# Eight-layer graph network on one core: layer norm by node tile, tied weight loads, stores within a recurrence and by tile

## The chip, the cores and the metric

The kernel runs on one core of a Trainium2 chip, as one launch. Its time is the device time in microseconds. Before the change the median of three runs is 5691.67 us (5687.64 to 5693.42). One further execution was profiled; every duration below is from that one.

The core has five engines with an instruction stream each, worked off in order: PE (matrix products, with PEld loading its weights), DVE (vector), ACT (scalar functions), POOL and SP. SP, ACT and POOL also issue DMAs, which run on 16 DMA engines; SP and ACT have a hardware queue each, POOL a software queue. A tensor in on-chip memory has up to 128 partitions; matrix products are written to PSUM.

## The reference

x is 625 x 512 (float32), with a graph of 20000 edges sorted by destination. Eight layers follow one another, each as

```
x = x + layer(_layernorm(x))      # (x - mean) / sqrt(var + 1e-5), no scale, no shift
```

with these layers:

- l0_gnn: Chebyshev graph convolution, eight terms through a dense 625 x 625 Laplacian.
- l0_ffn: one of 16 experts, picked by the mean over all nodes.
- l1_gnn: graph convolution of width 128, gathered over the edges, then 128 to 512.
- l1_ffn: 8 experts, gates by eight Sinkhorn rounds, each expert for its top nodes.
- l2_gnn: 32 relations made of 8 bases; `h_rel = einsum('ni,rio->rno', x, weight)`, then gathered over the edges.
- l2_ffn: a recurrence over the 625 nodes as time steps:

```
logits = concat(h, c, x_t) @ W_sel.T + b_sel
s = argmax(logits)                                # one of S = 4 weight sets
g = x_t @ W_ih[s].T + h @ W_hh[s].T + b_ih[s] + b_hh[s]
i, f, g, o = split(g, 4)
c = sigmoid(f) * c + sigmoid(i) * tanh(g);  h = sigmoid(o) * tanh(c)
```

- l3_gnn: two layers of graph attention with four heads, then a linear layer.
- l3_ffn: attention over the nodes with 8 heads, in one of three variants picked by the mean over the nodes.

## The kernel before

**Tiles.** The 625 nodes are NT = 5 tiles of P = 125 partitions. x stays on chip as `self.x`, 125 x 5 x 512. The stages run in the order of the layers; a scheduler orders the instructions of each engine by their dependences and puts in the semaphores. A DMA takes one of 8 semaphores in turn and waits for the DMA that had it last. Three loops (edge counts, the two gathers of l1_gnn and l2_gnn, the recurrence) are ordered by hand in a `tile_critical` block. At the beginning of such a block every engine waits for all DMAs that stand ahead of it in the program, whatever they load.

**Layer norm.** `layer_norm` (L39 to L55) stands at the head of each layer: bn_stats and bn_aggr for each tile (DVE, L46, L47), one square root for all five tiles (ACT, L48), one reciprocal (L49), then a subtract and multiply for each tile (L51). Its tiles come from a pool of the layer. After it `transpose_nodes` (L57) turns the nodes by 20 PE transposes (L63), copied from PSUM by DVE (L64). l0_ffn and l3_ffn also take the mean over nodes by 40 small products (L373, L1276).

**Loads on ACT's queue.** l1_ffn issues the 8 bases of l2_gnn, 1 MB each, from ACT at its beginning (L471). l2_gnn issues 16 small DMAs of comb from ACT (L588).

**l2_gnn.** It multiplies xT by the 8 bases (L608), brings the result into another layout by node_basis DMAs (L619), multiplies it by comb (L634) and stores the relation table to DRAM by 40 stores on SP (L643, L647). The gather (L681 on) is a `tile_critical` block: POOL issues 160 indirect loads of 125 table rows (L688), DVE makes a one-hot matrix for each (L692), PE adds up (L216). Then x is added (L700).

**Loads of the recurrent weights.** Memory for four sets of W_hh, 4 MB each (whh0 to whh3), is set aside ahead of the gather (L660). `load_set` (L703) loads a set by four DMAs of 1 MB. Sets 0 to 2 go by SP, drawn from a generator among the stores of gin. whh3 first serves as the double buffer of W_ih (`load`, L747 to L752): each column block of W_ih is 2 MB, two DMAs from ACT. Set 3 itself is loaded at the end by POOL, half after each of the last two column blocks. None of these loads depends on the relation table, so the scheduler puts them as early as memory and semaphores allow.

**gin** (l2_ffn, L779 to L877) computes the input products of all four sets for all nodes. It has 8 column blocks times 5 tiles, 40 units. A unit is 16 products and two of the bias on PE (L847, L849) into one of three PSUM buffers, then ACT's sigmoid and tanh for the cell's guess (L812 to L815), and a split of the sum into three bf16 parts: ACT casts (L737), DVE subtracts (L738), ACT casts (L739), DVE subtracts (L740). The parts stand in gxo3 (pool of three buffers) and go to DRAM as gxp, 750 KB for each unit, by SP (L860). PE transposes the guess of unit u - 1 after the products of unit u (L824). At the end, the logits' part of the input (xl3) is stored to gxp from ACT, five DMAs of 19 KB (L878). Padding zeros of gxp are stored by POOL in `setup` (L92).

**Recurrence** (L891 to L1097): a `tile_critical` block of 625 steps. SP loads a row of gxp for each step (L1092) into gs, PE adds it and h times W_hh[s] (L955, L964), DVE and ACT compute the cell.

**End.** `store` (L281) writes x to `out` by one DMA on SP.

The lines of the steps that follow are these; the scheme of a unit of gin is the heart of it:

```
ps = psum.tile([P, 2, D], F32, name="gx_ps")
...
rest = p2.tile([P, 2, 2, 256], F32, name="rest", bufs=1)
o3 = p3.tile([P, 3, 2, 2, 256], BF16, name="gxo3")
summands(lambda q: o3[:, q].rearrange("p s q n -> p q s n"),
         ps.rearrange("p q (s n) -> p q s n", n=256), rest)
nc.sync.dma_start(gxp[t * P : (t + 1) * P, c // 2, :, at : at + 2 * D],
                  o3.rearrange("p r s q n -> p r (s q n)"))
```

Of the kernel before, what the change touches and what calls it, by code (L numbers as in the profile page):

```python
# [8 lines left out]
F32 = mybir.dt.float32  # L9
# [20 lines left out]
class _Kernel:  # L30
# [8 lines left out]
    def layer_norm(self, pool):  # L39
        nc, x = self.nc, self.x  # L40
        st = pool.tile([P, NT, 6], F32, name="ln_st")
        mv = pool.tile([P, NT, 2], F32, name="ln_mv")
        rs = pool.tile([P, NT], F32, name="ln_rs")
        xn = pool.tile([P, NT, D], F32, name="ln_x")
        for t in range(NT):
            nc.vector.bn_stats(st[:, t, :], x[:, t, :])  # L46
            nc.vector.bn_aggr(mv[:, t, :], st[:, t, :])  # L47
        nc.scalar.activation(rs, mv[:, :, 1], AF.Sqrt, bias=self.eps)  # L48
        nc.vector.reciprocal(rs, rs)  # L49
        for t in range(NT):  # L50
            nc.vector.tensor_scalar(  # L51
                xn[:, t, :], x[:, t, :], mv[:, t, 0:1], rs[:, t : t + 1],
                op0=ALU.subtract, op1=ALU.mult,
            )
        return xn  # L55
# [11 lines left out]
    def setup(self, ctx):  # L67
# [7 lines left out]
        self.eps = const.tile([P, 1], F32, name="eps")  # L75
        nc.vector.memset(self.eps, 1e-5)
# [10 lines left out]
        zero = const.tile([P, DC - 1, 3, 26], BF16, name="zero")  # L87
        nc.gpsimd.memset(zero, 0.0)
        self.graph()
        for t in range(NT):  # L90
            for j in range(1, DC):
                nc.gpsimd.dma_start(self.gxp[t * P : (t + 1) * P, j, :, 2048:], zero[:, j - 1])  # L92

    def graph(self):
# [53 lines left out]
        with tc.tile_pool(name="graph", bufs=1) as pool, tc.tile_pool(  # L148
# [38 lines left out]
            for t in range(NT):  # L187
                nc.scalar.copy(self.count[:, t, :512], main[t])
# [92 lines left out]
    def store(self):  # L281
        self.nc.sync.dma_start(self.out.rearrange("(t p) c -> p t c", p=P), self.x)


    def l0_gnn(self):
        tc, nc, a, x = self.tc, self.nc, self.a, self.x
        K = 8
        with ExitStack() as ctx:
# [3 lines left out]
            xn = self.layer_norm(pool)  # L292
# [33 lines left out]
            for k in range(K - 1, -1, -1):  # L326
# [10 lines left out]
                for t, ps in enumerate(sums):  # L337
# [6 lines left out]
                    if k == 0:  # L344
                        nc.vector.tensor_add(x[:, t, :], ps, x[:, t, :])
                    elif k == 1:
# [11 lines left out]
    def l0_ffn(self):  # L358
        tc, nc, a, x = self.tc, self.nc, self.a, self.x
        NE = 16  # L360
        with tc.tile_pool(name="sw", bufs=1) as pool, tc.tile_pool(
# [6 lines left out]
            xn = self.layer_norm(pool)  # L368
# [33 lines left out]
            for t in range(NT):  # L402
                ps = psum.tile([P, D], F32, name="y_ps")
                for c in range(DC):
# [4 lines left out]
                                               op0=ALU.mult, op1=ALU.add)  # L409


    def l1_gnn(self):
        tc, nc, a, x = self.tc, self.nc, self.a, self.x
        H = 128
        with tc.tile_pool(name="gc", bufs=1) as pool:
# [8 lines left out]
            xn = self.layer_norm(pool)  # L424
# [23 lines left out]
            with tc.tile_pool(name="gc_ps2", bufs=2, space=PSUM) as psum, tc.tile_pool(  # L448
                name="gc2", bufs=2
            ) as p2:  # L450
                for t in range(NT):
# [7 lines left out]
                    nc.vector.tensor_add(x[:, t, :], ps, x[:, t, :])  # L459

# [111 lines left out]
    def l2_gnn(self):  # L572
# [88 lines left out]
        with tc.tile_pool(name="rs", bufs=1) as pool:  # L661
# [7 lines left out]
            with tc.tile_pool(name="rel_in", bufs=1) as sp, tc.tile_pool(  # L669
# [29 lines left out]
                for t in range(NT):  # L699
                    nc.vector.tensor_add(x[:, t, :], acc[t], x[:, t, :])  # L700
# [759 lines left out]
```

## Time and profile before

| what | value |
|---|---|
| median of three runs | 5691.67 us (5687.64 to 5693.42) |
| the profiled execution | 5684.2 us |
| its span | 5682.4 us |
| mean granted TensorE clock | 0.952 of full speed |
| PE busy | 5001.1 us (88%) |
| DVE busy | 2527.0 us (44%) |
| ACT busy | 957.8 us (17%) |
| POOL busy | 422.5 us (7%) |
| first gate product of the recurrence | 1971.58 us |
| first addition of its result to x | 5102.87 us |

Times of the timeline count from the start of the span. A row of the timeline is: start, duration (us), engine and line, operation, output <- inputs, shapes, count, and in brackets the idle time before it with what ended that. A row of waits is: who waited (engine, tile, line) <- for whom, us in all, times, the longest. A row of a stretch is: its bounds, its length, busy time of PE with its instructions, the granted clock, the busy share of the DMA engines, and GB/s. A row of a group is: busy us, mean ns of one, then the idle time of the engine ahead of it with what ended it. PE counts as busy while it works at half clock too.

### The profile page before, as it was taken

Reading aid. Unit: us, or ns where it says so; the run is one execution under the profiler, and the core shown is the slowest. Engines: PE = TensorE matmul, PEld = TensorE weight load, DVE = VectorE, ACT = ScalarE, POOL = GpSimd, SP = SyncE. Lnnn points to the kernel's source line nnn. Section 1 sums busy time; section 2 is a strip of 40 time slices with the busy share of each in tenths; the row PEclk is TensorE's granted clock in tenths of the full one; section 3 lists DMA queues with packets and bytes.
Section 4 is the critical chain, followed back from the end, with each engine's and each line's share of the span. In section 5 each row is a group of like instructions: output and inputs, shape, how many; then the busy total and the mean of one; then the engine's idle time right before and its main releaser. Section 6 shows DMA issues by size and latency. Waiting matters only on the chain.

```text
span 5682.4 us, 173043 instructions
## 1 busy us (share of the span) xinstructions
PE 5001.1 (88%) x74317; PEld 3028.8 (53%) x74318; DVE 2527.0 (44%) x10296; ACT 957.8 (17%) x3300; POOL 422.5 (7%) x361
## 2 busy tenths in 40 slices
PE   6898879885799789898999999999999898988987
PEld 2444764321244356565666666666666565665544
DVE  6312436334333344444444454444545444456514
ACT  1000001120023211111111111111111111114314
POOL 1000760006700000000000000000000000000000
PEclk8798998988999899999999999999999999998989
DMA  1100121396554400000000000000000000001000
GB/s 15 46 30 14 41 67 66 93 286 172 152 143 156 116 10 11 10 11 10 11 10 10 10 11 11 11 10 11 11 11 11 11 10 10 9 23 49 15 32 10
DMA packets 153754, 247.87 MB, mean 44 GB/s; under 512 B 58875, under 2 KB 61572, under 8 KB 151462
## 3 DMA queue, kind: packets, MB, share of 16 engines
q1 hardware_dynamic: 83850, 163.27, 9.6%
q0 software_dynamic: 50288, 56.13, 4.0%
q10 hardware_dynamic: 19372, 25.52, 1.6%
q8 instruction: 115, 1.88, 0.1%
q14 instruction: 129, 1.06, 0.1%
HBM read 160.50 MB, written 73.72 MB: 41 GB/s over the span
## 4 chain that ended last, share of the span: by engine, by line
PE 53%; DVE 6%; issue 3%; DMA 2%; PEld 1%; ACT 1%; PEldq 0%; SPq 0%; ACTq 0%; DVEq 0%
PE gate_if L964 21%; PE gate_o L964 9%; PE gate_g L964 9%; DVE to L1076 3%; PE gate_if L955 3%; PE idle L972 2%; DMA gs<-gxp 2%; PE o_ps L1203 2%; PE o_ps L1137 2%; PE big_ps L1312 1%; PE gate_g L955 1%; PE gate_o L955 1%; PE big_ps L1332 1%; PE fc_ps L1243 1%; PE blk_ps L1193 1%
## 5 line engine op out<-in xcount | busy, mean ns | idle before, releaser
L964 PE MATMUL gate_if<-whh,h 128*32 128x256 f32 x21664 | 1348.6, 387 | 2.1 <-issue 2.1
L964 PEld LDWEIGHTS gate_if<-whh,h 128*32 128x32 f32 x21664 | 599.8, 109 | 368.3 <-DVE h L1080 129.2
L964 PE MATMUL gate_g<-whh,h 128*32 128x128 f32 x19968 | 672.2, 275 | 0.0
L964 PE MATMUL gate_o<-whh,h 128*32 128x128 f32 x19968 | 659.2, 273 | 0.0
L1067 DVE STREAM_TRANSPOSE tif<-gate_if 128x256 f32<-128x256 f32 x625 | 281.3, 450 | 837.7 <-PE gate_g L964 834.0
L964 PEld LDWEIGHTS gate_g<-whh,h 128*32 128x32 f32 x19968 | 520.8, 110 | 171.6 <-issue 162.6
L964 PEld LDWEIGHTS gate_o<-whh,h 128*32 128x32 f32 x19968 | 557.7, 110 | 0.0
L1059 ACT ACTIVATE sd<-tif 128x8 f32<-128x8 f32 x625 | 134.7, 216 | 2120.1 <-DVE tif L1067 2120.1
L955 PE MATMUL gate_if<-gs,pick 128*128 128x256 bf16 x678 | 192.7, 284 | 135.5 <-DVE to L1076 47.1
L847 PE MATMUL gx_ps<-whh,xT 128*125 128x512 f32 x640 | 299.9, 612 | 0.3 <-DVE xls L787 0.3
L216 PE MATMUL acc<-msg,dst_w 125*125 125x512 f32 x352 | 193.8, 659 | 105.0 <-DMA msg<-rel_table,row_i 95.3
L1068 DVE STREAM_TRANSPOSE tg<-gate_g 128x128 f32<-128x128 f32 x625 | 198.0, 317 | 160.2 <-PE gate_g L964 160.2
L258 PE MATMUL acc<-msg,dst_w 125*125 125x128 f32 x1600 | 210.7, 282 | 44.0 <-DMA msg<-conv_table,src_i 37.8
L250 POOL DMA_INDIRECT msg<-conv_table,src_i x160 | 196.1, 1226 | 609.3 <-issue 607.2
L688 POOL DMA_INDIRECT msg<-rel_table,row_i x160 | 195.9, 1224 | 537.5 <-issue 519.6
L1076 DVE STREAM_TRANSPOSE to<-gate_o 128x128 f32<-128x128 f32 x625 | 198.1, 317 | 67.1
L258 PEld LDWEIGHTS acc<-msg,dst_w 125*125 125x125 f32 x1600 | 188.3, 190 | 66.4 <-issue 55.2
L1024 PE MATMUL logits<-gs,three 128*2 128x5 bf16 x624 | 103.5, 166 | 129.0 <-issue 50.0
L1088 DVE MAX8 mx<-logits 2x8 f32<-2x8 f32 x624 | 100.8, 162 | 246.4 <-PE logits L1036 246.4
L972 PE MATMUL idle<-hot 128*128 128x384 bf16 x624 | 204.8, 328 | 0.0
L1024 PEld LDWEIGHTS logits<-gs,three 128*2 128x2 bf16 x624 | 49.3, 79 | 289.7 <-DMA gs<-gxp 229.8
L216 PEld LDWEIGHTS acc<-msg,dst_w 125*125 125x125 f32 x352 | 59.1, 198 | 240.6 <-issue 191.3
(356 smaller groups left out, 6150.9 us busy)
## 6 DMA issues: line engine op xcount, KB each, us to landing
rel_table<-h_rel SPq DMA_DIRECT2D x39, 1024.0 KB
gs<-gxp SPq DMA_DIRECT2D x625, 48.6 KB
gxp<-gxo SPq DMA_DIRECT2D x40, 750.0 KB
whh<-in_L_ffn_W_ih ACTq DMA_DIRECT2D x16, 1024.0 KB
whh<-in_L_ffn_W_hh SPq DMA_DIRECT2D x12, 1024.0 KB
node_basis<-by_basis SPq DMA_DIRECT2D x39, 256.0 KB
ch_wk<-in_L_gnn_weight SPq DMA_DIRECT2D x8, 1024.0 KB
expert<-in_L_ffn_experts SPq DMA_DIRECT2D x8, 1024.0 KB
```

What stands on the lines that cost most here:

```text
L216: m = PE.matmul(out, lhs, rhs, start=False, stop=False, skip_group_check=True)
L250: nc.gpsimd.indirect_dma_start(out=m, out_offset=None, in_=table, in_offset=bass.IndirectOffsetOnAxis(ap=index[:, c : c + 1], axis=0),)
L258: nc.tensor.matmul(acc[t][:, :width], w1[:, t * P : (t + 1) * P], m, start=c == 0, stop=c == EC - 1)
L688: get = nc.gpsimd.indirect_dma_start(out=msg[:, i, :], out_offset=None, in_=table, in_offset=bass.IndirectOffsetOnAxis(ap=idx[:, c : c + 1 ...
L847: nc.tensor.matmul(ps[:, q], xT[:, k, t * P : (t + 1) * P], w[:, q, k, :], start=k == 0, stop=False)
L955: m = PE.matmul(out[:, : hi - lo], pick, gs[:, s * D + lo : s * D + hi], start=True, stop=last, skip_group_check=True)
L964: yield PE.matmul(out[32 * j : 32 * j + 32, : hi - lo], h[:, b : b + 1].to_broadcast([128, 32]), self.whh[s][:, b, j, lo:hi], start=False, ...
L972: PE.matmul(idle[:, :cols], hot[:, :128], hot[:, :cols], start=True, stop=True)
L1024: after(PE.matmul(lg[:, :LG], three[:, 0], gs[:, S * D : S * D + LG], start=True, stop=False), s_gx, rows)
L1067: after(DVE.transpose(tif, IF[:, :256]), s_if, t + 1).then_inc(s_v)
L1068: after(DVE.transpose(tg, G[:, :128]), s_g, t + 1).then_inc(s_v)
L1076: after(DVE.transpose(to, O[:, :128]), s_o, t + 1).then_inc(s_v)
```

## The change

- `layer_norm` becomes `norm(t)`, for one tile, with one square root and one reciprocal each. It is called in the layer ahead, right after the addition that completes x of that tile; the five of the first layer are called within `graph`. Its tiles are allocated once, for the whole kernel.
- The padding zeros are stored in l1_ffn by the source. In the order of POOL's instructions they stand where they stood.
- Two small DMAs read the end of the relation table into whh3 (from ACT) and whh0 (from SP), ahead of the loads into these sets, so that those loads can only follow the table's last stores.
- In gin, `rest` uses the memory of xn, and gxo3 has two buffers.
- Set 3 of W_hh is loaded by ACT's queue instead of POOL's.
- The logits' part xl3 is stored from POOL within the recurrence's block; each store waits for the one before, and SP waits for a tile's store before it loads that tile's first row.
- The output is stored by tile, after each tile's last addition.
- In l1_ffn, three instead of two held expert results are added after each product of a later expert.

```diff
-    def layer_norm(self, pool):
...
+    def norm(self, t):
+
         nc, x = self.nc, self.x
+        st, mv, rs = (v[:, t] for v in self.moments)
+        nc.vector.bn_stats(st, x[:, t, :])
+        nc.vector.bn_aggr(mv, st)
+        nc.scalar.activation(rs, mv[:, 1:2], AF.Sqrt, bias=self.eps)
         nc.vector.reciprocal(rs, rs)
+        nc.vector.tensor_scalar(self.xn[:, t, :], x[:, t, :], mv[:, 0:1], rs, op0=ALU.subtract, op1=ALU.mult)
...
                     if k == 0:
                         nc.vector.tensor_add(x[:, t, :], ps, x[:, t, :])
+                        self.norm(t)
...
-                for _ in range(2):
+                if e == NE - 1:
+                    self.norm(t)
+                for _ in range(3):
...
+        nc.scalar.dma_start(self.whh[3][0:1, :, 0, :2], table[N * R - 1 :, : 2 * DC].rearrange("p (q n) -> p q n", q=DC))
+        nc.sync.dma_start(self.whh[0][:, 0, 0, :1], table[N * R - 128 :, :1])
...
-                p3 = gin.enter_context(tc.tile_pool(name="gin3", bufs=3))
+                p3 = gin.enter_context(tc.tile_pool(name="gin3", bufs=2))
...
-                        rest = p2.tile([P, 2, 2, 256], F32, name="rest", bufs=1)
+                        rest = self.xn[:, :2].rearrange("p q (s n) -> p q s n", n=256)
...
-                        list(self.load_set(S - 1, slice(2 * (c % 2), 2 * (c % 2) + 2), nc.gpsimd))
+                        list(self.load_set(S - 1, slice(2 * (c % 2), 2 * (c % 2) + 2), nc.scalar))
...
-                for t in range(NT):
-                    nc.scalar.dma_start(gxp[t * P : (t + 1) * P, 0, :, 4 * D :], xl3[:, :, t])
-            hist = self.recurrence(ctx, wl, gxp)
+            hist = self.recurrence(ctx, wl, gxp, xl3)
...
+            for t in range(NT):
+                d = nc.gpsimd.dma_start(gxp[t * P : (t + 1) * P, 0, :, 4 * D :], xl3[:, :, t])
+                if t:
+                    after(d, s_xl, 16 * t)
+                d.then_inc(s_xl, 16)
             for t in range(N):
+                if t % P == 0:
+                    SP.wait_ge(s_xl, 16 * (t // P + 1))
                 d = SP.dma_start(gs[: 3 * DC, :], gxp[t].rearrange("j q g -> (j q) g"))
...
                 nc.vector.tensor_add(x[:, t, :], ps[:, :D], x[:, t, :])
+                nc.sync.dma_start(self.out[t * P : (t + 1) * P, :], x[:, t, :])
```

The calls of `norm(t)` in the other layers follow the last addition to x in the same way (L408, L459, L700, L885, L1246 of the kernel before).

## Prediction

> **What bounds the kernel now.** I read the chain of work that ended last first, then the costliest groups, to learn which engine the time hangs on.
>
> ```profile
> PE 53%; DVE 6%; issue 3%; DMA 2%; PEld 1%; ACT 1%; PEldq 0%; SPq 0%; ACTq 0%; DVEq 0%
> ...
> L964 PE MATMUL gate_if<-whh,h 128*32 128x256 f32 x21664 | 1348.6, 387 | 2.1 <-issue 2.1
> ...
> L847 PE MATMUL gx_ps<-whh,xT 128*125 128x512 f32 x640 | 299.9, 612 | 0.3 <-DVE xls L787 0.3
> ```
>
> The end hangs on TensorE. L964 is the recurrence, 1971.6 to about 5100 us; none of its steps is edited, so 3130 us stay as they are. The gain or loss must come from the 2550 us around it. There I asked for the waits of PE between 1036 and 1260 us and, in a second answer, between 512 and 600 us:
>
> ```profile
> PE tr_ps L63 <- DVE ln_x L51: 11.3, 1, 11.3
> ```
>
> ```profile
> PE tr_ps L63 <- ACT dinv L275: 7.1, 1, 7.1
> ...
> PE mean_ps L373 <- DVE ln_x L51: 5.9, 1, 5.9
> ```
>
> Each is PE standing idle (us in all, times, longest) while a layer norm runs between the last addition to x and the next layer's transposes. The timeline of DVE shows how the longest comes about:
>
> ```profile
> 1035.35 0.75 DVE L560 SCALAR_TENSOR_TENSOR x<-y_ps,sel,x 125x512 f32<-125x512 f32 x1 [2.68 <-PE y_ps L491]
> 1036.02 0.68 DVE L46 BATCH_NORM_STATS2 ln_st<-x 125x6 f32<-125x512 f32 x1
> ...
> 1045.71 0.19 DVE L49 RECIPROCAL ln_rs<-ln_rs 125x5 f32<-125x5 f32 x1 [6.09 <-ACT ln_rs L48]
> 1045.93 2.37 DVE L51 TENSOR_SCALAR ln_x<-x,ln_mv,ln_rs 125x512 f32<-125x512 f32 x5
> ```
>
> x is complete at 1036.1, but the one square root stands on ACT behind 16 DMA issues of comb (1037.0, 8.3 us) and the statistics of all five tiles.
>
> **1. Layer norm by tile.** The order of instructions of the changed kernel puts four of the five tiles' norms beside the previous layer's matmuls. Behind the last x there remain statistics 0.66, aggregate 0.17, root 0.30, reciprocal 0.19, scaling 0.5 and two handovers between engines: an estimate of 2.3 us. Layer by layer, from the idle time of PE and the copies that DVE must still do:
> - l0_ffn: PE starts at 512.2 and is busy to 522. Now the last scaled tile is there at about 509, and four tiles' transposes fill the wait: **-5**.
> - l1_gnn: PE starts at 566.0 after 7.1 idle and works through 20 transposes and 40 matmuls to 576.4. It can start at 559.0, and its own 10.6 us of work then end near 569.6: **-6.5**.
> - l1_ffn: the root waits behind 8 issues of bases (838.9, 13.6 us); PE starts at 853.8 after 14.9 idle. In the new order the roots precede most issues; DVE's five additions and norms (1.9 us each from 834.3) and four copies end near 846, while PE has transposes from 840: **-11**. The cost moved is that bases 3 to 8 are issued later; they are first read at 1052.7, 200 us on.
> - l2_gnn: last tile ready at 1039.2 (copies between), matmuls on bases at 1041 in place of 1052.7: **-11.5**. Fifteen comb issues now come after the roots and end about 1047; the first reader comes only after 1080.
> - l2_ffn: DVE is the limit on both sides (five additions and norms are 9.4 us from 1567.0, to 1577; before, the last scaling ended at 1576.7): **-1**.
> - l3_gnn: DVE again: in the new order counts and negations stand between the norms, and adding up its rows from 5101.3 gives the last copy at 5121 against 5120.7: **0**.
> - l3_ffn: the 40 mean matmuls (8.5 us) end at 5461.7, now near 5456.5: **-5**.
> - l0_gnn: its norm hid in DVE's idle time at 186 to 194 us. Four statistics, three aggregates, two reciprocals and two scalings (3.9 us) now precede the graph stage, on a DVE chain from 18.1 to 28.6 that starts it; that chain has some 2.5 us of gaps: **+2**.
>
> Together **-38**. The bounds are -26 (half of the two large ones) and -44. The four extra roots and reciprocals of each layer lie beside matmuls. Here the clock matters too:
>
> ```profile
> 1046.00:1050.00 4.00, 2.95 (x13) 0.50 0.10 1
> 1050.00:1054.00 4.00, 3.23 (x11) 0.50 0.00 0
> 1054.00:1058.00 4.00, 4.00 (x7) 0.66 0.00 0
> 1058.00:1062.00 4.00, 4.00 (x10) 1.00 0.00 0
> ```
>
> The column ahead of the last two (DMA share, GB/s) is the granted clock: after the idle stretch PE works about 10 us at half speed, and the 17 matmuls from 1052.7 take 9.55 us, where 17 x 0.43 = 7.3 would do. I count nothing for this, since gaps of 2 to 3 us remain. The Trainium skill (TensorE: Matmul & The Clock Gate, "What's actually happening") has the clock halved after an idle window of about 3.4 us and restored after as long a busy one; the rows agree with a halving, and by its window most of the shortened gaps would keep the clock.
>
> **2. Ties of the loads.** W_ih's four loads (4 MB, ACT) were issued from 1268.2, ahead of the table's landing at about 1276.7. DVE and POOL enter the gather at 1302.5, held by those loads and two W_hh loads of SP; in the new order this barrier still holds for all of them. Their transfer starts some 5 to 7 us later, behind a small DMA that waits for the table. One W_hh load (5 us) has no tie and fills that time, the DMAs were at a share of 1.0 before too, and the second W_hh load no longer waits for the first W_ih: **+1.5**. Ends: -2 (a freer table) and +6 (the whole delay). The zero stores stand at the same place of POOL's order: 0.
>
> **3. Two gxo3 buffers in place of three.** Behind 40 units of 8.4 us of matmuls (L847, to 1939.5) ACT waits 39.5 us in 13 times for the landing of a store, so that three buffers were already short:
>
> ```profile
> 1730.24 0.38 ACT L813 ACTIVATE th<-gx_ps 125x256 bf16<-125x256 f32 x1
> 1741.40 1.01 ACT L737 CAST gxo<-gx_ps 125x1024 bf16<-125x1024 f32 x1 [10.78 <-DMA gxp<-gxo]
> ```
>
> Behind this waiting cast stand the cell's tanh and product, and PE's transpose waits for those 5.83 us, until 1743.93. A store of 750 KB takes 6.6 us (116 GB/s, DMA share 0.33, at 1928 to 1936); a buffer is held for 4.6 (write) + 2.3 (issue to first packet) + 6.6 = 13.5 us, under two units' 16.8. Alone, two buffers would do, with 3.3 us to spare. But from 1637 to 1800 the same queue carries five W_hh loads of about 5 us, and W_ih's 2 MB per column (8 us of all DMAs) slow it. PE's lead over the queue shrinks by one unit, 8.4 us, in each burst that uses it up; and when ACT waits, the queue runs dry for 4.6 + 2.3 - 6.6 = 0.3 us per unit, about 13 times. One burst: 8.4 + 4 = **+13** (rounded up, since the first loads come one store earlier in the new order). Ends: 0 (bursts stay inside the 3.3) and +25 (a second and third burst). The Trainium skill (DMA: Bandwidth & Descriptors, "Why a DMA increments its semaphore by 16 and not by 1") speaks against the change: a DMA from SP or ACT is spread over the largest number up to 16 that divides the slowest dimension, 5 for 125 rows. The share of 0.33 agrees with 5 of 16, so a store gains nothing from idle DMAs.
>
> **4. Start of the recurrence.**
>
> ```profile
> 1946.19 0.29 DVE L740 TENSOR_TENSOR xl<-less,xl 125x125 bf16<-125x125 f32 x1 [0.36 <-ACT xl L739]
> 1966.06 0.17 DVE L924 TENSOR_REDUCE quarter<-ident 128x4 f32<-128x12 f32 x1 [19.58 <-DMA gxp<-xl]
> ```
>
> Last gx matmul 1939.5, barrier 1966.1, first gs load 1969.5, first gate 1971.6. The barrier no longer holds for the logits' stores, but for the last gxo store and the W_hh set. Four W_hh issues on ACT (0.5 to 1 us each) now stand between the last unit's casts, so the last store is written near +9 after the last matmul and shares the DMAs with 2 MB: landed at +19 in place of +26.6. Then POOL's first store (about 2.4 from the barrier to its issue, as SP's row shows, and 6.2 to land, the median of the 15 zero stores of the same 19 KB on POOL) holds SP's first load: +28, against +30. **-1.5**; ends -8 and +5. The later four stores land within 40 us and are needed only every 125 steps of 5 us.
>
> **5. Output by tile.** The one store is issued at 5669.5 and ends the span at 5682.4: 12.9 us, at 128 GB/s. The additions are 3.4 us apart, a tile needs 250 KB / 128 GB/s = 2.0 us, so nothing queues up; the last one ends in 12.9 - 10.2 + 2.0 = 4.7, at most 6.9 after its issue: **-6** (ends -8, -4).
>
> **Sum**: -38 + 1.5 + 13 - 1.5 - 6 = -31. The profiled execution took 5684.2 (span 5682.4), giving 5653. The median of the runs is 5691.67, 7.5 above it, so I put the forecast at 5661.
>
> **The rivals.**
> - *Gin hides it, and the clock stays up.* Stores of 13.5 us fit into 16.8, and four of the gaps no longer lose some 2 us each to the cold clock (9.55 - 7.3 above): part 3 at 0 and -8 beside: 5640. For it: outside 1637 to 1800 ACT never waits. Against: 13 waits with three buffers. By the Trainium skill's window, cited above, the clock part would come out so.
> - *Given back downstream.* Half the gain of part 1 vanishes since l1_ffn has 11.6 us of idle PE later anyway (waiting for DVE at 984 to 996) and the table's stores run at a DMA share of 0.9: -31 + 19 = -12: 5680. Against: the chain in l1_ffn is DVE's, and it starts earlier too.
> - *Slower: two buffers throttle the whole saturated stretch.* If a store's 14 to 20 us from write to landing (units 5 to 22) come from crowded DMAs and not from its own queue, a pair of units takes 4.6 + 20 = 24.6 against 16.8: 17 x 3.9 = +66 instead of +13, 5714. It decides from +44 on, 1.1 us per unit. Against it: the stores run end to end there, as a queue does.
>
> **How the numbers follow.** Forecast (5661, own range 5648 to 5674) 0.55; first rival 0.22; given back 0.15; slower 0.08. The range reaches over the bounds of gin and of part 1: 5638 to 5684. A measurement of this kernel can tell about 0.2% from no change, 11.4 us. Faster takes the first two cases and a third of the third: 0.82; same 0.10; slower 0.08.
>
> **What would show it.** PE's wait for the norm at 1036 and 839 down to 2 to 4 us; ACT's wait for gxp<-gxo well above 39.5 us and PE's losses in gin at some 20 us; first gate 28 us behind the last gx matmul; the gather starting 25 to 27 us behind the table's landing; last store to the end 5 to 7 us. Wrong would be gin at above 40 or the l1_ffn and l2_gnn gains gone at their layers' ends.

## The result and the profile after

| | before | changed |
|---|---|---|
| median of six runs each, us | 5689.66 (5680.5 to 5693.42) | 5664.9 (5656.6 to 5670.12) |
| ratio, 95% interval | | 0.996 [0.995, 0.9971] |
| profiled execution, span, us | 5684.2, 5682.4 | 5670.12, 5668.3 |

The change is worth 0.4% (0.29 to 0.5), 25 us by the medians, against a forecast of 31 us (5661). The profiled execution of the changed kernel is the longest of its six, that of the kernel before lies under its median: the spans are 14 us apart, the medians 25. A stage differs by some us from one execution to the next of the same work (first to last gate of the recurrence: 3126 to 3139 us over the profiles below that leave its work alone), so the table shows where time went, and the ratios what an edit is worth. Line numbers from here on are those of the changed kernel; the rows of another kernel carry its own.

The page of the changed kernel, its chain of waits and two of its costliest groups:

```profile
PE 72%; DVE 8%; DMA 7%; issue 7%; POOL 3%; ACT 1%; PEld 1%; PEldq 0%; SPq 0%; ACTq 0%; POOLq 0%; DVEq 0%
...
L962 PE MATMUL gate_if<-whh,h 128*32 128x256 f32 x21664 | 1349.9, 387 | 3.2 <-issue 3.2
...
L847 PE MATMUL gx_ps<-whh,xT 128*125 128x512 f32 x640 | 308.2, 625 | 6.7 <-DVE xn L740 6.5
```

The chain is followed through 99% of the span here and through 66% before, so its shares are not compared; both name PE. The recurrence's products take 387 ns each as before; those of gin are longer by 13 ns (625 against 612) and wait more. Stage by stage, from the timelines (length of each stage in us):

| stage, from mark to mark | before | changed | difference | forecast |
|---|---|---|---|---|
| start to last x of l0_gnn | 506.4 | 507.8 | +1.5 | +2 |
| l0_ffn, to its last x | 52.6 | 46.2 | -6.4 | -5 |
| last x to first gather product of l1_gnn | 27.4 | 21.0 | -6.4 | -6.5 |
| gather of l1_gnn, to last x | 252.7 | 256.4 | +3.6 | 0 |
| l1_ffn: last x to first Sinkhorn sum | 31.3 | 15.2 | -16.1 | |
| l1_ffn: first Sinkhorn sum to its last x | 165.0 | 178.3 | +13.3 | -11 with the row above |
| last x to first product on bases (l2_gnn) | 17.3 | 5.7 | -11.7 | -11.5 |
| to the issue of the table's last store | 216.1 | 214.6 | -1.4 | 0 |
| to the first load of the gather | 34.4 | 32.1 | -2.3 | +1.5 |
| gather, head of l2_ffn, to first gx matmul | 283.1 | 284.8 | +1.7 | -1 |
| gin: first to last gx matmul | 353.0 | 368.5 | +15.6 | +13 |
| to first gate | 32.4 | 33.9 | +1.5 | -1.5 |
| recurrence, first to last gate | 3129.0 | 3135.2 | +6.2 | 0 |
| l3_gnn, to last x | 345.0 | 346.3 | +1.3 | 0 |
| l3_ffn, to last x | 223.2 | 216.5 | -6.7 | -5 |
| to the end of the span | 13.6 | 5.9 | -7.7 | -6 |

The waits of PE at the head of l2_gnn, and below them those at the heads of l1_gnn and l0_ffn (engine and line that waited, what it waited for: us in all, times, longest):

```profile
PE tr_ps L55 <- DVE x L556: 0.8, 1, 0.8
...
PE tr_ps L55 <- DVE xn L47: 0.7, 1, 0.7
```

```profile
PE tr_ps L55 <- DVE x L399: 0.8, 1, 0.8
PE mean_ps L364 <- DVE x L335: 0.8, 1, 0.8
```

The waits of 11.3, 7.1 and 5.9 us are gone. The timeline of DVE at the end of l1_ffn shows the new order:

```profile
1024.83 0.75 DVE L556 SCALAR_TENSOR_TENSOR x<-y_ps,sel,x 125x512 f32<-125x512 f32 x1 [0.63 <-PE y_ps L487]
1025.62 0.70 DVE L43 BATCH_NORM_STATS2 ln<-x 125x6 f32<-125x512 f32 x1
...
1027.60 0.15 DVE L46 RECIPROCAL ln<-ln 125x1 f32<-125x1 f32 x1
1027.83 0.68 DVE L56 COPY xT<-tr_ps 128x500 f32<-128x500 f32 x1
1028.43 0.54 DVE L47 TENSOR_SCALAR xn<-x,ln,ln 125x512 f32<-125x512 f32 x1
```

From the last x (1025.6) to the last scaled tile (1029.0) it is 3.4 us, where it was 12.2, and copies of transposed tiles lie between the steps of the last norm. The third change in the numbers is in gin. ACT's waits there, first in the changed kernel and then in experiment 1 below, which has a third gxo3 buffer again (its third part of the buffers goes by the name xn):

```profile
ACT gxo L739 <- DMA gxp<-gxo: 52.9, 18, 5.7
```

```profile
ACT gxo L739 <- DMA gxp<-gxo: 31.5, 10, 11.1
...
ACT xn L739 <- DMA gxp<-xn: 9.0, 4, 3.0
```

In the changed kernel ACT waits 52.9 us for stores instead of 39.5, more often (18 against 13) and at most 5.7 at a time instead of 10.8. Last, the new start of the recurrence, by the timeline of POOL and the waits of SP:

```profile
1958.46 1.33 POOL L1090 DMA_DIRECT2D gxp<-xl  x1 [407.83 <-issue]
1962.69 1.31 POOL L1090 DMA_DIRECT2D gxp<-xl  x1 [2.90 <-DMA gxp<-xl]
```

```profile
SPq L1097 <- DMA gxp<-xl: 4.6, 1, 4.6
```

The last gx matmul starts at 1930.5, POOL issues its first store 28.0 us later, and SP's first load of a row waits 4.6 us for that store. The first gate comes at 1964.4.

### The profile page after: what moved, and what is told of

It reads as the page before. It is cut to its first block, busy times and chain, and to the rows that moved or that the text cites. A ratio compares the mean times of both kernels' runs of the same rounds, so it can differ in the third digit from the quotient of the medians.

```text
span 5668.3 us, 173121 instructions
## 1 busy us (share of the span) xinstructions
PE 5005.0 (88%) x74317; PEld 3024.8 (53%) x74318; DVE 2526.8 (45%) x10328; ACT 966.0 (17%) x3331; POOL 427.3 (8%) x358
## 4 chain that ended last, share of the span: by engine, by line
PE 72%; DVE 8%; DMA 7%; issue 7%; POOL 3%; ACT 1%; PEld 1%; PEldq 0%; SPq 0%; ACTq 0%; POOLq 0%; DVEq 0%
PE gate_if L962 21%; PE gate_o L962 9%; PE gate_g L962 9%; PE gx_ps L847 4%; DVE to L1074 3%; PE gate_if L953 3%; PE ch_b L332 3%; PE ch_b L323 2%; PE y_ps L604 2%; POOL msg L687 2%; DMA gs<-gxp 2%; PE idle L970 2%; DMA gxp<-gxo 2%; PE cnt L209 2%; PE o_ps L1208 2%
## 5 line engine op out<-in xcount | busy, mean ns | idle before, releaser
L243 POOL DMA_INDIRECT msg<-conv_table,src_i x160 | 196.3, 1227 | 598.0 <-issue 594.6
L251 PEld LDWEIGHTS acc<-msg,dst_w 125*125 125x125 f32 x1600 | 187.9, 189 | 67.7 <-issue 58.2
L847 PEld LDWEIGHTS gx_ps<-whh,xT 128*125 128x125 f32 x640 | 117.9, 195 | 138.7 <-issue 131.5
```

The costliest lines, as they stand in the source:

```text
L243: nc.gpsimd.indirect_dma_start(out=m, out_offset=None, in_=table, in_offset=bass.IndirectOffsetOnAxis(ap=index[:, c : c + 1], axis=0),)
L251: nc.tensor.matmul(acc[t][:, :width], w1[:, t * P : (t + 1) * P], m, start=c == 0, stop=c == EC - 1)
L847: nc.tensor.matmul(ps[:, q], xT[:, k, t * P : (t + 1) * P], w[:, q, k, :], start=k == 0, stop=False)
```

## The experiments

All ratios are to the kernel before, timed on the same chip. Theory throughout: the norm by tile and the output by tile gain, two buffers lose, and l1_ffn gives back most of its share. The rivals say that the time hangs elsewhere (the clock, other loads, the place of the calls). Each diff is against the changed kernel.

**1. A third gxo3 buffer,** in the part of xn's memory that gin does not use.

```diff
-                        o3 = p3.tile([P, 3, 2, 2, 256], BF16, name="gxo3")
+                        if (c * NT + t) % 3 == 2:
+                            o3 = self.xn[:, 2:].rearrange("p t n -> p (t n)").bitcast(BF16).rearrange(
+                                "p (r s q n) -> p r s q n", r=3, s=2, q=2)
+                        else:
+                            o3 = p3.tile([P, 3, 2, 2, 256], BF16, name="gxo3")
```

> The changed kernel with three gxo3 buffers again (every third unit uses the part of xn that is free in gin). In the changed kernel the stretch from the first to the last gx matmul takes 368.5 us, 15.6 more than before. Theory (two buffers stall ACT and, through the transposes, PE): the stretch returns to 352 to 356 us, ACT's wait for gxp<-gxo falls from its value in the changed kernel to about the 39.5 us of before, and the time falls by 11 to 16 us, to about 5651. Rival (the stretch is longer because loads of W_hh and W_ih fall into other places of the queue): it stays at 364 or more and the time falls by under 5.

Measured: 5643.03 us, ratio 0.9929 [0.9916, 0.9943]. Gin took 353.6 us, 14.9 less than in the changed kernel, and was back at the 353.0 of before. So the missing buffer is the whole loss of gin; the other edits of the stage (set 3 on ACT, later loads) cost nothing there that this shows.

**2. The loads of bases on POOL's queue** instead of ACT's. This was to tell why l1_ffn lost 13.3 us between its first Sinkhorn sum and its end. The timeline of PE in the changed kernel:

```profile
862.75 2.27 PE L510 MATMUL small_ps<-gates,ones 125*125 125x8 f32 x10 [1.22 <-DVE gates L517]
866.24 2.26 PE L510 MATMUL small_ps<-gates,ones 125*125 125x8 f32 x10 [1.22 <-DVE gates L517]
869.73 2.27 PE L510 MATMUL small_ps<-gates,ones 125*125 125x8 f32 x10 [1.22 <-DVE gates L517]
873.22 1.41 PE L531 MATMUL row_ps<-ident,gates 125*125 125x125 f32 x5 [1.22 <-DVE gates L517]
874.42 28.92 PE L487 MATMUL y_ps<-expert,xT 128*125 128x512 f32 x64
903.18 0.71 PE L531 MATMUL row_ps<-ident,gates 125*125 125x125 f32 x5
```

The Sinkhorn rounds (L510) run alone, with 1.22 us of waiting in each. The 64 expert products stand in one lump behind them, ahead of seven of the eight groups of products that turn the gates into rows (L531). DVE then waits for those rows: in its waits between 840 and 985 us,

```profile
DVE scratch L538 <- ACT row L535: 22.4, 2, 20.2
```

In the kernel before, the expert products stood between the rounds:

```profile
881.46 3.68 PE L491 MATMUL y_ps<-expert,xT 128*125 128x512 f32 x8
884.98 1.16 PE L514 MATMUL small_ps<-gates,ones 125*125 125x8 f32 x10
```

ACT copies these products to memory (L496), and with the head of the layer earlier, its issues of bases reach up to those copies. On the chip they do not hold them up (the issues are done at 843.0, and the first copy, at 844.5, waits for PE); what changed is the order that the scheduler laid down.

```diff
-            nc.scalar.dma_start(self.bases[:, b], a["L2_gnn_bases"][b].rearrange("(c p) o -> p c o", p=128))
+            nc.gpsimd.dma_start(self.bases[:, b], a["L2_gnn_bases"][b].rearrange("(c p) o -> p c o", p=128))
```

> The changed kernel with the 8 loads of bases issued from POOL instead of ACT, which in the order of instructions puts four early products of the experts between the Sinkhorn rounds again. In the changed kernel the first Sinkhorn sum on PE is 23.8 us earlier than before, but the expert choice (sel times gates) only 13.3 us. Theory (the scheduler put 32 early products behind the rounds, since ACT's copies stand behind its bases issues; DVE then waits 20 us for a row behind them on PE): the choice comes 8 to 11 us earlier again and the time falls by 8 to 11 us, to about 5655. Rival (DVE's ranking is bound by PE's products wherever they stand): the choice moves by under 3 us and so does the time.

Measured: 5653.81 us, ratio 0.9935 [0.9922, 0.9949]. The choice of the top nodes (the last product of sel and gates) comes 15.3 us earlier than in the changed kernel, more than expected, and the layer's end 16.1. The products stand between the rounds again:

```profile
851.45 1.16 PE L510 MATMUL small_ps<-gates,ones 125*125 125x8 f32 x10
852.47 3.68 PE L487 MATMUL y_ps<-expert,xT 128*125 128x512 f32 x8
855.98 1.16 PE L510 MATMUL small_ps<-gates,ones 125*125 125x8 f32 x10
```

A round's ten products take 1.16 us instead of 2.27: the granted clock is the other half of the matter (last section). So the loss in l1_ffn is the order of these instructions, and the place of the issues changes it. It isn't the only thing that does: experiment 5 restores the order with the loads on ACT. By what rule the scheduler chooses is not in the trace.

**3. Two held results** added after each later product, as before, in place of three.

```diff
-                for _ in range(3):
+                for _ in range(2):
```

> The changed kernel with two instead of three held expert results added after each product of a later expert. Theory (the third held addition delays the release of PSUM and PE starts its later products later: from the choice to the last addition of x 53.3 us in place of 50.5 before): this stretch returns to 50 to 51.5 us and the time falls by 2 to 3 us. Rival (the stretch grew by the norms that now follow the additions): it stays at 53 and the time within 1 us.

This kernel leaves something out: the last held results are added after the norm of their tile was taken, so l2_gnn works on other numbers, and the recurrence takes another course. Its time is not comparable (5695.84 us, ratio 1.0022 [1.0013, 1.0031]). The stretch from the choice to the last x took 50.2 us, against 52.8 with three and 50.0 before. So the third addition costs 2.6 us in its place; with it all held results of a tile are added before the norm that l1_ffn calls.

**4. The loads not tied** to the table's end: the two small DMAs at L658 and L659 left out.

```diff
-        nc.scalar.dma_start(self.whh[3][0:1, :, 0, :2], table[N * R - 1 :, : 2 * DC].rearrange("p (q n) -> p q n", q=DC))
-        nc.sync.dma_start(self.whh[0][:, 0, 0, :1], table[N * R - 128 :, :1])
```

> The changed kernel without the two DMAs that tie the loads to the table's end. The forecast had put the tie at a loss of 1.5 us; in the traces, from the last table store's issue to the first gather instruction, the change gained 2.3 us (34.4 to 32.1). Theory (free of W_ih's loads, the table's last stores land sooner and the loads then run one kind after the other, which costs nothing in all): without the tie the stretch is 34 to 35 us again and the time 1.5 to 3 us longer. Rival (the gain came from elsewhere, as the place of the W_hh loads): the stretch stays at 32 and the time within 1 us.

Measured: 5655.81 us, ratio 0.9952 [0.9939, 0.9966]. From the issue of the table's last store to the gather it is 34.4 us, as before the change, against 32.1 with the ties (31.3 to 32.9 in all nine profiles that have them). So the ties gain 2.3 us in their place. In the total the two kernels can't be told apart: the intervals overlap, and the middle is even lower without the ties.

**5. The norm's calls at the head** of each layer, still one root for each tile; eight places of this form:

```diff
                         nc.vector.tensor_add(x[:, t, :], ps, x[:, t, :])
-                        self.norm(t)
...
-            xn = self.xn
+            for t in range(NT):
+                self.norm(t)
+            xn = self.xn
```

> The changed kernel with all five norms of a layer at its head again (still one root and one reciprocal for each tile); everything else as changed. In the changed kernel PE's first work of a layer comes, behind the last addition to x, at +0.7 us (l0_ffn), +4.0 (first product of l1_gnn), +2.2 (l1_ffn, first gate product), +5.7 (bases of l2_gnn) and +1.2 (l3_ffn). Theory (the gain of the change is the norms beside the layer ahead): these become about 6, 11, 10 to 19, 12 to 17 and 7, and the time is 22 to 35 us longer than the changed one, about that of the kernel before. Rival (most of part 1 was given back within the layers): the time is under 15 us longer.

Measured: 5659.5 us, ratio 0.9956 [0.9942, 0.997]. The expected loss of over 20 us did not come in the total, and the stages show two things that cancel. The waits of PE for the norm at the heads stayed at 0.8 to 1.6 us but for l2_gnn's:

```profile
PE tr_ps L55 <- DVE xn L47: 7.2, 1, 7.2
```

A norm that needs one tile only is for the most part taken forward by the scheduler, wherever the call stands. But in l1_ffn and l2_gnn the last roots now stand behind ACT's issues:

```profile
839.27 0.67 ACT L45 ACTIVATE ln<-ln,eps 125x1 f32<-125x1 f32 x3 [13.33 <-DMA bases<-in_L_gnn_bases]
...
1017.38 0.29 ACT L45 ACTIVATE ln<-ln,eps 125x1 f32<-125x1 f32 x1 [10.94 <-DMA comb<-in_L_gnn_w_comp]
```

The first Sinkhorn sum comes 22.5 us behind the last x instead of 15.2, the first product on bases 12.6 instead of 5.7: 14 us lost. Against that, the expert products stand between the Sinkhorn rounds again, though the loads of bases are still ACT's, and from the first Sinkhorn sum to the last x of l1_ffn it is 159.3 us instead of 178.3. So the place of the call does count in two layers, and the unchanged total does not show it.

**6. Set 3 of W_hh on POOL's queue,** as before.

```diff
-                        list(self.load_set(S - 1, slice(2 * (c % 2), 2 * (c % 2) + 2), nc.scalar))
+                        list(self.load_set(S - 1, slice(2 * (c % 2), 2 * (c % 2) + 2), nc.gpsimd))
```

> The changed kernel with set 3 of W_hh loaded by POOL's queue again. In the changed kernel the first gate follows the last gx matmul by 33.9 us (32.4 before), against a forecast of 28. Theory (the last gxo store, issued 11 us behind the last matmul, shares the DMAs with 2 MB of W_hh whichever queue they are on; on POOL's it starts later still): 36 to 41 us, the time 2 to 6 us longer. Rival (ACT's issues ahead of the last units' casts delay that store): 30 to 32 us and the time 2 to 4 us shorter.

Measured: 5656.62 us, ratio 0.9951 [0.9938, 0.9965]. The last gx matmul to the first gate took 30.0 us instead of 33.9: ACT's issues do hold up the last units' parts. Gin itself is 363.6. The total doesn't part it from the changed kernel.

**7. The logits' stores ahead of the recurrence's block,** from ACT, as before.

```diff
+                for t in range(NT):
+                    nc.scalar.dma_start(gxp[t * P : (t + 1) * P, 0, :, 4 * D :], xl3[:, :, t])
...
-            for t in range(NT):
-                d = nc.gpsimd.dma_start(gxp[t * P : (t + 1) * P, 0, :, 4 * D :], xl3[:, :, t])
...
-                if t % P == 0:
-                    SP.wait_ge(s_xl, 16 * (t // P + 1))
```

> The changed kernel with the logits' stores ahead of the recurrence on ACT again, without SP's waits for them. In the changed kernel POOL issues the first store only 3 us behind the barrier and SP's first load waits 4.6 us for it; the barrier itself comes with the last gxo store and W_hh. Theory (the wait moved from ahead of the barrier to behind it and is about as long): first gate 32 to 35 us behind the last gx matmul, the time within 3 us. Rival (the stores within the recurrence gain what the 19.6 us wait of before showed): 38 us or more and the time 4 to 8 us longer.

Measured: 5660.87 us, ratio 0.996 [0.9947, 0.9974]; last gx matmul to first gate 34.4 us against 33.9. Moving these stores into the block gains nothing: the block's start waits for the last gxo store anyway.

**8. Edits 1 and 2 together.**

> The changed kernel with three gxo3 buffers and the bases issued from POOL, the two edits that gained by themselves (ratio to the kernel before 0.9929 and 0.9935 against 0.996 for the changed kernel). Theory (they lie in different stretches, so the gains add up): ratio 0.9904, about 5633 us. Rival (loads of bases or the shorter gin collide with something later): 0.992 or more.

Measured: 5627.18 us, ratio 0.9898 [0.9883, 0.9913]. The product of the single ratios, 0.9929 x 0.9935 / 0.996, is 0.9904: the two add up. Gin 355.1 us, layer l1_ffn ended at 1006.6.

**9. One root for five tiles,** at the head of each layer, with everything else as changed (tiles of the norm for the whole kernel, too). Against experiment 5 it tells the number of roots from the place of the call.

```diff
-    def norm(self, t):
+    def norm_all(self):
...
+        for t in range(NT):
+            nc.vector.bn_stats(st[:, t], x[:, t, :])
+            nc.vector.bn_aggr(mv[:, t], st[:, t])
+        nc.scalar.activation(rs[:, :, 0], mv[:, :, 1], AF.Sqrt, bias=self.eps)
+        nc.vector.reciprocal(rs[:, :, 0], rs[:, :, 0])
```

> The changed kernel with the norm at the head of each layer and one root and one reciprocal for all five tiles, as before; the tiles are still those of the whole kernel. With the calls alone at the head again, the scheduler still put four tiles' norms beside the layer ahead, and the time stayed (ratio 0.9956). Theory (the one root is what binds the norms to the last tile): PE waits again for 5 to 7 us at the heads of l0_ffn, l1_gnn and l3_ffn and over 7 at l2_gnn; since gin's two buffers (+15.6) and the rest (-6) remain, the ratio to the kernel before is 1.000 to 1.003. Rival (it is the layer's pool that bound them, and tiles of the whole kernel are enough): waits of 1 to 3 us and a ratio under 0.998.

Measured: 5684.79 us, ratio 1.0002 [0.9993, 1.0011]: the whole gain of the change is gone. PE's wait at l2_gnn is back at 11.0 us, and ACT's timeline has the reason again:

```profile
1036.04 8.45 ACTq L584 DMA_DIRECT2D comb<-in_L_gnn_w_comp  x16
1044.54 0.30 ACT L45 ACTIVATE ln<-ln,eps 125x5 f32<-125x5 f32 x1 [76.49 <-DMA comb<-in_L_gnn_w_comp]
```

The root that needs all five tiles can't be issued ahead of the last x, and then it stands behind 16 issues on ACT. What binds all five norms to the last tile is the single root: with the calls in the same place it is 1.0002 here and 0.9956 in experiment 5. The order of PE in l1_ffn is no part of this, since the expert products stand between the rounds in both. The root is not the whole of it in three layers: at l0_ffn, l1_gnn and l3_ffn PE waits 3.5, 3.1 and 3.0 us for the norm, where 5 to 7 were expected and the kernel before had 5.9, 7.1 and 6.8. About half of those waits stays away with one root. The timelines of DVE at l0_ffn, first before the change and then here, show how:

```profile
506.98 1.28 DVE L46 BATCH_NORM_STATS2 ln_st<-x 125x6 f32<-125x512 f32 x2
...
511.54 2.37 DVE L51 TENSOR_SCALAR ln_x<-x,ln_mv,ln_rs 125x512 f32<-125x512 f32 x5
```

```profile
507.00 0.69 DVE L43 BATCH_NORM_STATS2 ln<-x 125x6 f32<-125x512 f32 x1
...
508.90 2.37 DVE L48 TENSOR_SCALAR xn<-x,ln,ln 125x512 f32<-125x512 f32 x5
```

Before, the statistics of all five tiles followed the last x (506.4), and the scaling began 5.2 us behind it. Here only the last tile's do, the other four lie beside l0_gnn, and it begins 2.8 us behind (506.1). So the rival is right in part. That the tiles of the whole kernel free these statistics is likely, as little else of the norm differs from before, but no run has them as the one change.

**10. The loads tied to the gather's end:** four numbers of x, after the gather is added, are written into each set ahead of its loads.

```diff
-        nc.scalar.dma_start(self.whh[3][0:1, :, 0, :2], table[N * R - 1 :, : 2 * DC].rearrange("p (q n) -> p q n", q=DC))
-        nc.sync.dma_start(self.whh[0][:, 0, 0, :1], table[N * R - 128 :, :1])
...
                     nc.vector.tensor_add(x[:, t, :], acc[t], x[:, t, :])
+                    if t == 0:
+                        for s in (3, 0, 1, 2):
+                            nc.vector.tensor_copy(self.whh[s][:P, :, 0, 0], x[:, 0, :DC])
```

> The changed kernel with the loads of W_ih and W_hh tied to the gather's end (a copy of four numbers of x into each set, behind the first addition of the gathered sums) instead of the table's end. Theory (the gather waits at its barrier for 6 MB that nothing there needs; the 22 us between the gather's last product and the first gx product hide the first W_ih block): the gather begins 7 to 10 us behind the last table store's issue in place of 32, the first gx product comes 22 to 27 us behind the gather's last product, gin is 0 to 10 us longer as two more W_hh loads fall into it, and the time is 12 to 22 us shorter than the changed kernel's: ratio 0.992 to 0.994. Rival (the loads' time comes back at the first gx product or in gin): the time is within 4 us of the changed one.

Measured: 5643.58 us, ratio 0.9929 [0.9915, 0.9942]. POOL's first gather load, in the changed kernel and in this one:

```profile
1277.20 1.50 POOL L687 DMA_INDIRECT msg<-rel_table,row_i  x1 [460.85 <-issue]
```

```profile
1249.58 1.48 POOL L685 DMA_INDIRECT msg<-rel_table,row_i  x1 [435.83 <-issue]
```

The table's last store is issued at 1245.1 and 1240.7: 32.1 and 8.9 us ahead. Some 23 us of the barrier were loads that the gather does not need. After the gather these loads cost 0.9 us up to the first gx matmul, which is within what that stretch varies (279.5 to 284.8 us over the profiles without this edit), and 3.6 us in gin (372.1).

**11. Edits 1, 2, 6 and 10 together.**

> The changed kernel with three gxo3 buffers, bases on POOL, set 3 of W_hh on POOL, and the loads tied to the gather's end. Theory (the stretches are apart; with three buffers the two further loads in gin cost less): ratio 0.9898 of the first two edits, less 0.0007 for set 3 and 0.002 to 0.004 for the tie: 0.985 to 0.987, about 5605 us. Rival (gin's queue of SP is full with two more loads and takes the gain back): 0.989 or more.

Measured: 5612.77 us, ratio 0.9879 [0.9864, 0.9894], with experiment 12 the shortest kernel here, and 1.2% under the kernel before. The gains over the changed kernel add up to a ratio of 0.9864 (0.996 less 0.0031, 0.0025, 0.0009 and 0.0031); a bit is missing. Gin took 362.6 us, where 355.1 + 3.6 - 4.9 = 353.8 would be the sum.

**12. The same without edit 6,** to find what is missing.

> The version with four edits, with set 3 of W_hh back on ScalarE's queue. Open: its gin (first to last gx matmul) took 362.6 us, where the sum of the single edits is 355.1 (third gxo3 buffer and bases on POOL) + 3.6 (loads behind the gather) - 4.9 (set 3 on POOL) = 353.8. Theory: set 3 on POOL costs in gin once three buffers are there, since its 2 MB then start early and share the DMAs with the last units' stores instead of following them; gin then falls to 356 to 359 here, last gx matmul to first gate stays at 30 to 31, and the ratio to the kernel before is 0.986 to 0.9875. Rival: it is the loads moved behind the gather that cost it (W_hh's sets 0 to 2 all queue up with the stores of gin): gin stays at 361 to 364, the start is 30 to 31, ratio 0.988 to 0.989.

Measured: 5614.36 us, ratio 0.9879 [0.9862, 0.9895]; gin 364.0 us, start 30.7. The rival holds: set 3's queue makes no difference that can be told here, and it is the loads moved behind the gather. Experiment 8 differs from this kernel by the tie alone, and its gin is 8.9 us shorter. Two of the twelve W_hh loads of SP ran ahead of the gather there, and five behind the first gx matmul, the last 154 us into gin; here it is none and ten, the last at 217 us, beside W_ih and the stores. ACT's waits for stores rose with it from 39.4 (31.3 and 8.1) in experiment 8 to 66.1 (46.6 and 19.5) here.

## Why the prediction was right, and where it was not

The forecast of 5661 against 5664.9 and its sign were right, and so were most steps. By the table l1_ffn missed its term by 8.2 us, the start of the recurrence by 3.0 and gin by 2.6, all three to the slow side; the ties came out 3.8 us better, and l0_gnn, l0_ffn, l3_ffn and the output 5.3 us together. (l2_ffn's -1 against +1.7 is left out, as its stage varies by 5 us.) That some 14 us of misses met 9 of the other sign, and the time came within 4 us of the forecast, is in part luck.

1. **Layer norm by tile, -38.** l0_gnn, l0_ffn, the head of l1_gnn, l2_gnn and l3_ffn came within 2 us of their terms (table above). The step that failed is the third: "DVE's five additions and norms [...] end near 846, while PE has transposes from 840: -11". The head gained even more, 16.1 us to the first Sinkhorn sum, but I followed the bases issues only to their first reader 200 us on, and did not read how the order of PE's instructions in the rounds had changed with them. The expert products went behind the rounds, and 13.3 us came back; the layer kept -2.8. This is the rival *given back downstream* in one layer, by a cause that I had not named: PE's 11.6 us of idle time later in the layer, which I had named, stayed what it was (11.5). Experiment 2 shows the cause, and its layer gains 19.0 us on the kernel before (177.3 against 196.3); experiment 5 shows the same order gained back in another way. Part 1 thus comes to about -32 by the table (l0_gnn +1.5, three heads -24.5, l1_ffn -2.8, l3_ffn -6.7). Experiment 9 prices the single root with the calls at the heads at 0.42% of the total, some 24 us, with an interval of about 8 us to each side (0.46% against experiment 5).
2. **Why the norm gains** was half told. I wrote that the order of instructions puts four norms beside the previous matmuls, and put it down to the edit as a whole; experiments 5 and 9 show that one root for each tile does most of it, and that the place of the call counts where issues on ACT come ahead of the last roots (l1_ffn and l2_gnn). At three smaller heads experiment 9 leaves about half to another cause.
3. **Ties, +1.5 with an end at -2.** It was -2.3, a little past the end that I called "a freer table", and by another way. I held that their transfer starts later and so ends later. W_ih's loads are issued 15.4 us behind the last store (0.5 ahead of it before), more than the 5 to 7 I took. But W_hh and W_ih then move one behind the other, and all together faster: 267 GB/s over the 29 us from 1246 to 1275, against 232 over the 32 us from 1270 to 1302 in the kernel before and 236 over 32 us (1243 to 1275) in experiment 4, which has the 34.4 us again. Why the mixed loads move less is not shown. The greater thing, that the barrier's loads as a whole cost some 23 us here, I saw in "this barrier still holds for all of them" and did not follow further, as the change leaves it.
4. **Two gxo3 buffers, +13.** It was +15.6, and 14.9 by experiment 1 alone. The size came from one burst of a lost unit plus 4 us of empty queue; ACT waited in more places and shorter than one burst would. So the size is confirmed, and the single burst is not. The slower rival (+66) is out.
5. **Start of the recurrence, -1.5.** It was +1.5: POOL's first store came 28.0 us behind the last gx matmul, where "landed at +19" and 2.4 more made 21.4; its landing took 4.0 instead of 6.2. (The "first gate 28 us behind" in the prediction's last part is its time of the first load; by its own sum the gate follows near +30.) So the landing of the last gxo store and of the W_hh set is the mis-sized term, by some 6.6 us. Experiment 6 shows 3.9 us of it as set 3 on ACT's queue among the last units; the rest I can't place.
6. **Output by tile, -6:** -7.7; last addition to the end took 5.9 us.
7. **The clock.** The rival *gin hides it, and the clock stays up* fails in its first half (experiment 1). The second half holds in part. At the head of l0_ffn the granted clock is 0.86 from 508 to 518, where it was 0.50 from 512 to 524. At l2_gnn it fell all the same (0.58 from 1030 to 1034), and the first 17 products on bases take 9.26 us instead of 9.55. In l1_ffn it fell where it had not before (last section).

The recurrence's +6.2 us is no part of the change that I can show: its 625 steps are unchanged but for the waits for xl, and with the very code of the change it took 3126.2 us in experiment 11 and 3138.7 in experiment 2. The same holds for the +3.6 us of l1_gnn's gather (experiment 12: 253.5).

## What to carry to other kernels

Give each tile its own small scalar step (root, reciprocal) if the step would else join all tiles: the scheduler can then take it forward, which it can't with one instruction that needs them all. See that no long row of DMA issues on the same engine comes ahead of it. Where an edit moves the head of a stage, read the order of all engines up to the stage's end: a scheduler may lay the later work out anew, as it did here by the place of the loads of bases (experiment 2) and by the place of the norm's calls (experiment 5). An unchanged total can hide a gain and a loss, so compare by stage. Loads that a block does not need are best tied to behind its beginning, but they come back where they then run, so look at what they meet there.

## What the runs showed of the hardware

**Half clock without a long gap.** In the changed kernel, by stretches of the Sinkhorn rounds (columns: stretch, its length, busy time of PE, PEld, DVE, ACT and POOL with the number of instructions, granted clock, DMA share, GB/s), and in experiment 2:

```profile
850.00:852.00 2.00, 1.45 (x12) 1.11 (x10) 0.44 (x3) 0.58 (x1) 0.00 (x0) 1.00 1.05 383
852.00:854.00 2.00, 1.33 (x9) 1.33 (x9) 0.55 (x3) 0.00 (x0) 0.00 (x0) 0.78 0.88 318
...
860.00:870.00 10.00, 6.33 (x30) 6.06 (x29) 2.98 (x15) 0.00 (x0) 0.00 (x0) 0.50 0.00 0
```

```profile
860.00:870.00 10.00, 10.00 (x43) 5.81 (x42) 1.99 (x10) 1.41 (x3) 0.00 (x0) 1.00 0.29 104
```

The granted clock fell between 852 and 854, and PE kept half speed though no gap from 840 to 874 was longer than 1.22 us. At half speed a round is 3.49 us and PE 63% busy; at full speed it would be an estimated 49% (1.16 us of products and 1.22 of waiting). The Trainium skill (TensorE: Matmul & The Clock Gate, "What's actually happening") has half rate after an idle window of about 3.4 us and full rate after a busy one as long. No such stretch was empty here, so a window that is partly busy can count as idle, and the rule can't be read as needing a gap of 3.4 us.

**W_hh's loads move at half the rate of W_ih's, both with the DMA engines busy.** In the changed kernel SP issues two W_hh loads at 1246.7 and 1255.4, and ACT the first W_ih load at 1260.5. So the first of these stretches has W_hh alone, and the second W_ih alone:

```profile
1256.00:1260.00 4.00, 0.00 (x0) 0.00 (x0) 2.49 (x5) 0.00 (x0) 0.00 (x0) 0.50 0.92 199
...
1265.00:1270.00 5.00, 0.00 (x0) 0.00 (x0) 0.00 (x0) 0.00 (x0) 0.00 (x0) 0.50 1.04 386
```

The DMA engines are nearly fully busy in both (0.92 and 1.04), and move 199 GB/s in the one and 386 in the other. In the kernel before, both kinds load at once:

```profile
1271.00:1280.00 9.00, 0.00 (x0) 0.00 (x0) 0.66 (x2) 0.00 (x0) 0.00 (x0) 0.50 1.03 250
1280.00:1290.00 10.00, 0.00 (x0) 0.00 (x0) 3.10 (x5) 0.00 (x0) 0.00 (x0) 0.50 1.03 203
1290.00:1297.00 7.00, 0.00 (x0) 0.00 (x0) 0.00 (x0) 0.00 (x0) 0.00 (x0) 0.50 1.05 276
```

That is between the two rates. So W_hh's low rate does not need a second queue beside it; it comes with these loads themselves. By the code each of them writes 32 partitions, and a load of W_ih 128. Whether that is the reason, no run here tests.
